# One Q projection per chunk for all four heads, spread to the heads' rows by way of DRAM

## The chip, the core and the metric

The kernel runs on one core of a Trainium2 chip. The metric is the device time of one execution in microseconds (us). Three runs of the kernel before took 6247.15, 6248.88 and 6250.07 us. A separate profiled execution gives the trace. The engines are called PE (TensorE), DVE (VectorE), ACT (ScalarE), POOL (GpSimd) and SP (SyncE, which issues nearly all DMAs).

## The reference

Two layers work on an image tensor of 4 images, 128 channels and 64 by 64 positions (4096 tokens an image).

```python
# layer 0: attention with 4 heads of 32 channels, residual, layer norm
Q, K, V = (split_heads(x_flat @ W + b) for W, b in ((Wq, bq), (Wk, bk), (Wv, bv)))
attn = softmax(einsum('bhnd,bhmd->bhnm', Q, K) * scale)
y = layernorm(einsum('bhnm,bhmd->bhnd', attn, V) @ Wo + bo + x_flat) * gamma + beta
# layer 1: the sum of three branches of y
spatial  = conv3x3(y) + bias
spectral = irfft2(channel_mix(rfft2(y)) + bias)
ym       = mamba(y)     # in_proj, causal conv of 4 taps, silu, a scan with 16 states, gate, out_proj
return spatial + spectral + ym
```

## The kernel before

**Tiling.** Tokens are handled in 32 chunks of 512 (8 an image). Attention goes by pairs of heads, so there are 64 halves H, each a chunk and a pair. A half takes 32 steps, one for each tile of 128 keys of the image, and a chunk 64 steps. The prediction calls these 64 steps a slot.

**One step of the hand-written loop.** For half H the kernel forms the scores of 128 keys against 512 queries (`scores_for_exp`, tile s, L478), subtracts the query's maximum by a matmul with `sel`, and takes the exponential on ACT (tile e, L486). The scores stand in one two-bank PSUM tile, so the matmuls of the next step wait until ACT has read it. In the same step PE forms scores of the next half for the running maximum (`scores_for_max`, L434, reduced by DVE into `part`, L441), seven steps ahead of their use, and multiplies the exponentials of the step before by V (`times_values`, L498).

**Precision.** Scores are single-pass matmuls of split numbers. Q is split into a high and a low part (tile Q, a [128, 2, 512] tile), K likewise. The rows of a pair are laid out as head, part, channel: two heads of 64 rows each, and within them 32 rows of K's high part and 32 of its low part. Q therefore has each head's 32 rows twice. The kernel before gets this layout from the weights: `wq_t` holds each head's columns twice, and one projection is made for each half.

**The Mamba scan** runs two chunks later, interleaved with attention. Every second step takes one vector of states: ACT makes the decay dA (L780), POOL the input term db (L785), DVE the scan hs (L793), and POOL copies the state, multiplies by C and accumulates (L796, L797, L812). The broadcast rows bc of B and C are loaded for each of the 16 states into three buffers (`scan_load`, L771).

**The planner.** All else (projections, convolution, gates, output) consists of generators, called jobs. A job is started by `plan.at(t, rank, job)` with the first step it may run. It asks for places by letters: P is a place for a matmul, D one on DVE, A one on ACT, B one of two spare PSUM banks; an empty string means only the next step. In the steady part an odd step has two places of P, D and A each, an even step a single place of A. Jobs are served by rank, then by their asked time. A job served earlier takes places from all behind it, so instructions of later jobs move to other steps.

**Jobs that the prediction names.** `project_q` makes Q (pq, L410; Q, L415 and L416). `project_kv` makes K and V of the next image (pk, L348; khi and klo; pv, L362; vst) and sends them by DRAM tiles kd and vd. `scan_dt` makes the step size: on ACT exponentials, logarithms and a bias (dt, spe, u, lnw), then on POOL three tensor operations (spe, dt, u, L738 to L740), and some steps later on ACT the scaling of xs by D (L747), which reads what the third POOL operation has read. `gate` makes the silu gate (pz, L756; zg). `scan_output` multiplies the accumulated scan by the gate on POOL (acc, L904) and, after two empty yields, projects it (py, L914). `flips` and `scan_output` add a mirrored image (L887).

[...]

Of the kernel before, what the change touches and what calls it, by code (L numbers as in the profile page):

```python
# [9 lines left out]
F32 = mybir.dt.float32  # L10
F32R = mybir.dt.float32r
AF = mybir.ActivationFunctionType
ALU = mybir.AluOpType
# [4 lines left out]
P = 128  # L18
W = 64
HEADS = 4  # L20
HD = P // HEADS
PAIRS = HEADS // 2
HS = P // 2
L = 512
# [131 lines left out]
def attention_then_conv_mamba(  # L156
# [38 lines left out]
    for h in range(HEADS):  # L195
        k, j = divmod(h, 2)
# [3 lines left out]
    for h in range(HEADS):  # L200
        k, j = divmod(h, 2)
        c = COL["bk"] + k
# [3 lines left out]
    Wk = wk_t.rearrange("c h d -> c (h d)")  # L206
    Wv = wat[:, 0, :]
    Wo = [wat[:, 1 + k, :] for k in range(PAIRS)]

    wq_t = const.tile([P, PAIRS, 2, 2, HD], F32, name="wq_t")  # L210
    bq = const.tile([P, PAIRS], F32, name="bq")
    for h in range(HEADS):
        k, j = divmod(h, 2)
        c = COL["bq"] + h
        for r in range(2):
            nc.scalar.dma_start(wq_t[:, k, j, r, :], wq[h, :, j * HS : j * HS + HD])
            nc.scalar.dma_start(
                bq[j * HS + r * HD : j * HS + (r + 1) * HD, k : k + 1],
                vecs[j * HS : j * HS + HD, c : c + 1],
            )  # L220
    Wq = [wq_t[:, k].rearrange("c j r d -> c (j r d)") for k in range(PAIRS)]
    nc.gpsimd.tensor_scalar(wq_t, wq_t, SCALE, None, ALU.mult)
    nc.gpsimd.tensor_scalar(bq, bq, SCALE, None, ALU.mult)
    cst = const.tile([P, K_SEL], F32, name="cst")
# [6 lines left out]
    for h in range(HEADS):  # L231
        row = h % 2 * HS
        hs = slice(h * HD, (h + 1) * HD)
# [19 lines left out]
    def col(name, k=0):  # L253
        return vec[:, COL[name] + k : COL[name] + k + 1]
# [5 lines left out]
    sel = const.tile([P, P], F32R, name="sel")  # L260
    ones = const.tile([P, 1], F32, name="ones")
    nc.vector.memset(ones, 1.0)
    minus_one = const.tile([P, 1], F32, name="minus_one")
    nc.vector.memset(minus_one, -1.0)
    g = const.tile([P, 3, P], F32, name="g")
# [53 lines left out]
    state = const.tile([P, NH * NS], F32, name="state")  # L319
# [5 lines left out]
    plan = Plan(2, {"x": 2, "f": 1})  # L325

    def bank_tile(bank, shape, name):
        return psum.tile(shape, F32, tag=f"m{bank}", name=name)


    def load_x(c, tag, bufs):
        t = att.tile([P, L], F32, tag=tag, name=f"{tag}_{c}", bufs=bufs)
        b, i = divmod(c, NCH)
        nc.sync.dma_start(t, x[b, :, i * L : (i + 1) * L])
        return t
# [61 lines left out]
    xqs = {}  # L397

    def load_q(c):
        yield ""  # L400
        xqs[c] = load_x(c, "xq", 2)

    def project_q(H):


        c, k = divmod(H, PAIRS)
        yield ""
        bank = yield "PB"
        pq = bank_tile(bank, [P, L], f"pq_{H}")
        nc.tensor.matmul(pq, Wq[k], xqs[c], start=True, stop=True)  # L410
        yield "DA"
        plan.release(bank, 2)
        q = att.tile([P, 2, L], F32R, tag="Q", name=f"Q_{H}", bufs=3)
        bias = bq[:, k : k + 1]
        nc.scalar.activation(q[:, 1, :], pq, AF.Identity, bias=bias)  # L415
        nc.vector.scalar_tensor_tensor(q[:, 0, :], pq, bias, q[:, 1, :], ALU.add, ALU.subtract)  # L416
        QT[H] = q


# [196 lines left out]
    def inner(c):  # L616
        return xps[c][:, 1 : RPC + 1, 1 : W + 1]

    def mamba_input(c):

        i = c % NCH
        while c not in XH:
            yield ""
        yield ""
        xp = loc.tile([P, RPC + 2, W + 2], F32, tag="xp", name=f"xp_{c}", bufs=2)
        xps[c] = xp
        nc.gpsimd.memset(xp[:, :, 0 : W + 2 : W + 1], 0.0)
        if i == 0:
            nc.gpsimd.memset(xp[:, 0, 1 : W + 1], 0.0)
            nc.gpsimd.memset(state, 0.0)  # L630
            nc.gpsimd.memset(carry, 0.0)
        if i == NCH - 1:
            nc.gpsimd.memset(xp[:, RPC + 1, 1 : W + 1], 0.0)
        bank = yield "PB"
        pt = bank_tile(bank, [P, TPC, P], f"pt_{c}")
        for t in range(TPC):
            nc.tensor.transpose(pt[:, t, :], XH[c][:, t, :], ident)
        yield "A"
        plan.release(bank)
# [127 lines left out]
    dA, db, bcs, scaled = {}, {}, {}, set()  # L767
# [19 lines left out]
    def scan_state(c, v):  # L787

        n, hf = divmod(v, NH)
        k = hf * NS + n  # L790
        assert (c, hf) in scaled
        hs = loc.tile([P, L], F32, tag="hs", name=f"hs_{c}_{k}")
        nc.vector.tensor_tensor_scan(  # L793
            hs, dA.pop((c, v)), db.pop((c, v)), state[:, k : k + 1], ALU.mult, ALU.add
        )
        nc.gpsimd.tensor_copy(state[:, k : k + 1], hs[:, L - 1 :])  # L796
        nc.gpsimd.tensor_tensor(hs, hs, bcs[c, n][:, 1, :], ALU.mult)  # L797
        if c >= CHUNKS - 2:

            if v == 0:  # L800
                late = psum.tile([P, NH, L], F32, tag=f"s{CHUNKS - c}", name=f"acc_{c}")
                for h in range(NH):
                    accs[c, h] = late[:, h, :]
            if n == 0:
                nc.tensor.matmul(accs[c, hf], ident, xss[c][hf], start=True, stop=False)
            nc.tensor.matmul(accs[c, hf], ident, hs, start=False, stop=n == NS - 1)  # L806
        elif n == 0:
            acc = loc.tile([P, L], F32, tag=f"acc{hf}", name=f"acc_{c}_{hf}")
            accs[c, hf] = acc
# [6 lines left out]
    def spectral(c):  # L816

        b, i = divmod(c, NCH)
        bank = yield "PB"
        p1 = bank_tile(bank, [P, TPC, P], f"p1_{c}")  # L820
        for t in range(TPC):
            nc.tensor.matmul(p1[:, t, :], XH[c][:, t, :], hilbert, start=True, stop=True)
        yield "A"
        plan.release(bank)
        hx = loc.tile([P, L], F32, tag="hx", name=f"hx_{c}", bufs=2)
        hxs[c] = hx
        nc.scalar.activation(
            hx, p1.rearrange("p t c -> p (t c)"), AF.Copy, scale=col("gamma")
        )
# [12 lines left out]
        if i == 0:  # L842
            wd[b] = dram.tile([P, N], F32, tag="wd", name=f"wd_{b}")
        nc.sync.dma_start(wd[b][:, i * L : (i + 1) * L], w)
# [106 lines left out]
    LEAD = 7  # L951
# [13 lines left out]
    plan.at(-4, 2, constants_of_the_rest())  # L965
    for H in range(HALVES):
        if H % PAIRS == 0:
            plan.at((H - 1) * NT - LEAD - 24, 0, load_q(H // PAIRS))
        plan.at((H - 1) * NT - LEAD - 14, 0, project_q(H))
        plan.at(H * NT - LEAD, 0, maxima(H))  # L970
        plan.at((H + 1) * NT + 1, 0, normalise(H, (H + 1) * NT + 9))
    for c in range(CHUNKS):
# [12 lines left out]
    while t < end or not plan.idle():  # L985
        H, m = divmod(t, NT)
# [5 lines left out]
        H, m = divmod(t - 1, NT)  # L992
# [3 lines left out]
        c, s = divmod(t - LAG, SLOT)  # L996
        odd = s % 2 == 1
        if -1 <= c < CHUNKS:
            v = c * STATES + s // 2
# [3 lines left out]
            else:  # L1003
# [8 lines left out]
                n = v // NH + 3  # L1012
# [87 lines left out]
```

## Time and profile before

| | |
|---|---|
| median of three runs | 6248.88 us |
| profiled execution, its own time | 6247.33 us |
| span of its trace | 6245.5 us |
| granted PE clock, mean | 0.978 |
| first exponential to last | 130.7 to 5967.6 us |
| instructions | 83489 |
| DMA bytes | 404.98 MB, 65 GB/s |

The first 130 us load weights, project K and V of the first image and find the first maxima. The main part has 2048 exponentials, so 2048 steps in 32 slots of 64. The last 280 us finish the scan and the output of the last chunks. The share of a busy engine is an average over these parts; what a change is worth is read from the step in which it lies. In the rows of groups, the numbers after the bar are the busy time, the mean of one instruction in ns, and the idle time of the engine just before them with what ended it. A two-pass f32 matmul shows as two records, so 64 projections are 128 records.

### The profile page before, as it was taken

The numbers are of one execution on the slowest core, as the hardware profiler recorded it, in microseconds if no ns is written. First come the engines' busy times: TensorE is split into PE (matmuls) and PEld (weight loads), VectorE is DVE, ScalarE is ACT, GpSimd is POOL, SyncE is SP. The second block draws the span as 40 slices with busy tenths as digits, with TensorE's granted clock in tenths as the row PEclk, the third lists the DMA queues.
The fourth block names the chain that finished last, engine by engine and source line by source line (L and its number), as shares of the span: only waits on it lengthen the run. The fifth ranks groups of instructions, "written<-read, shape, count | busy, mean of one in ns | idle before, by whom it ended". The sixth has DMA issues, their size and how long they took to land.

```text
span 6245.5 us, 83489 instructions
## 1 busy us (share of the span) xinstructions
PE 6001.6 (96%) x32076; PEld 2540.6 (41%) x32076; DVE 4284.2 (69%) x4405; ACT 3582.9 (57%) x4858; POOL 4605.3 (74%) x4951
## 2 busy tenths in 40 slices
PE   5999999999999999999999999999999999999956
PEld 2444444444444444444444444444444444444321
DVE  4556777777777677777767777767776766677556
ACT  1455666665666656566665556656565655665642
POOL 0006887777888777888887788877788877778866
PEclk7999999999999999999999999999999999999976
DMA  3002222223222222223232222222322222212223
GB/s 111 14 15 60 62 58 58 65 65 103 72 75 58 62 62 63 59 65 84 76 87 62 65 62 65 55 60 70 98 70 63 57 52 56 56 53 55 59 68 93
DMA packets 234225, 404.98 MB, mean 65 GB/s; under 512 B 38872, under 2 KB 40416, under 8 KB 233824
## 3 DMA queue, kind: packets, MB, share of 16 engines
q1 hardware_dynamic: 229440, 397.75, 23.3%
q8 instruction: 251, 4.11, 0.3%
q10 hardware_dynamic: 4384, 1.89, 0.1%
q14 instruction: 150, 1.23, 0.1%
HBM read 350.54 MB, written 49.02 MB: 64 GB/s over the span
## 4 chain that ended last, share of the span: by engine, by line
PE 80%; POOL 9%; DVE 5%; ACT 3%; issue 2%; DMA 1%; ACTq 0%; SPq 0%; POOLq 0%; DVEq 0%
PE po L498 27%; PE s L478 25%; PE s L434 13%; PE pf L857 4%; POOL hs L797 3%; DVE part L441 2%; ACT e L486 2%; DVE hs L793 2%; POOL db L785 1%; PE pi L663 1%; PE pdt L713 1%; POOL acc L812 1%; PE pq L410 1%; PE pd L699 1%; PE py L554 1%
## 5 line engine op out<-in xcount | busy, mean ns | idle before, releaser
L441 DVE TENSOR_REDUCE part<-s 128x2 f32<-128x1024 f32 x2048 | 2501.0, 1222 | 1613.6 <-PE s L434 1611.9
L486 ACT ACTIVATE e<-s 128x1024 f32<-128x1024 f32 x2048 | 2094.1, 1023 | 2257.5 <-PE s L478 2249.3
L498 PE MATMUL po<-e,V 128*33 128x512 f32 x8192 | 2160.1, 605 | 2.8 <-DVE oz L508 0.3
L478 PE MATMUL s<-Q,K 64*128 64x512 f32 x8192 | 1500.7, 444 | 25.3 <-ACT e L486 20.2
L793 DVE TENSOR_TENSOR_SCAN hs<-dA,state,db 128x512 f32<-128x512 f32 x1024 | 1305.7, 1275 | 158.9 <-ACT dA L780 69.2
L797 POOL TENSOR_TENSOR hs<-hs,bc 128x512 f32<-128x512 f32 x1024 | 1307.0, 1276 | 82.0
L434 PE MATMUL s<-K,Q 64*128 64x512 f32 x8192 | 1297.7, 395 | 44.4 <-DVE part L441 42.0
L478 PEld LDWEIGHTS s<-Q,K 64*128 64x128 f32 x8192 | 611.5, 185 | 1753.7 <-ACT e L486 1186.1
L785 POOL TENSOR_TENSOR db<-u,bc 128x512 f32<-128x512 f32 x954 | 1223.0, 1282 | 1.6 <-DMA bc<-bcd 1.6
L812 POOL TENSOR_TENSOR acc<-acc,hs 128x512 f32<-128x512 f32 x900 | 1151.7, 1280 | 70.6
L796 POOL COPY state<-hs 128x1 f32<-128x1 f32 x1024 | 212.6, 208 | 976.6 <-DVE hs L793 976.1
L434 PEld LDWEIGHTS s<-K,Q 64*128 64x128 f32 x8192 | 763.7, 186 | 280.5 <-DVE part L441 102.9
L478 PE MATMUL s<-MX,sel 64*128 64x512 f32 x4096 | 810.3, 392 | 0.0
L780 ACT ACTIVATE dA<-dt,negA 128x512 f32<-128x512 f32 x1024 | 702.5, 686 | 146.8 <-DVE hs L793 146.7
L498 PEld LDWEIGHTS po<-e,V 128*33 128x33 f32 x8192 | 299.2, 109 | 899.0 <-issue 865.0
L478 PEld LDWEIGHTS s<-MX,sel 64*128 64x128 f32 x4096 | 383.8, 184 | 90.0
L857 PE MATMUL pf<-xp,cw 128*128 128x512 f32 x576 | 288.2, 617 | 0.0
L450 POOL COPY wide<-mx 128x128 f32<-128x128 f32 x256 | 63.2, 292 | 196.9 <-DVE mx L447 196.9
L806 PE MATMUL acc<-hs,cst 128*128 128x512 f32 x128 | 110.8, 969 | 86.7 <-POOL hs L797 86.7
L531 POOL TENSOR_TENSOR oz<-oz,rz 128x512 f32<-128x512 f32 x64 | 81.9, 1279 | 106.7 <-DMA rz<-rd 106.7
L857 PEld LDWEIGHTS pf<-xp,cw 128*128 128x128 f32 x576 | 96.1, 188 | 131.9 <-issue 126.9
L554 PE MATMUL py<-wat_vo,oz 128*128 128x128 f32 x512 | 83.0, 285 | 22.6 <-POOL oz L531 18.6
(134 smaller groups left out, 3561.0 us busy)
## 6 DMA issues: line engine op xcount, KB each, us to landing
bc<-bcd SPq DMA_DIRECT2D x512, 512.0 KB
K<-kd SPq DMA_DIRECT2D x64, 256.0 KB
rz<-rd SPq DMA_DIRECT2D x128, 128.0 KB
vd<-vst SPq DMA_DIRECT2D x32, 264.0 KB
V<-vd SPq DMA_DIRECT2D x32, 264.0 KB
xq<-in_x SPq DMA_DIRECT2D x32, 256.0 KB
xk<-in_x SPq DMA_DIRECT2D x32, 256.0 KB
kd<-khi SPq DMA_DIRECT2D x32, 256.0 KB
```

Of the source, the lines that this page charges most:

```text
L434: nc.tensor.matmul(sc[:, j, :], QT[H][rows[j], n, t * P : (t + 1) * P], KK[k][m][rows[j], :], start=n == 0, stop=n == 1,)
L441: nc.vector.tensor_reduce(part[H][:, t, :, m], sc, AX.X, ALU.max)
L478: nc.tensor.matmul(s[:, j, :], sel[rows[j], :] if n == 2 else KK[k][i][rows[j], t * P : (t + 1) * P], mov[rows[j], :], start=n == 0, stop= ...
L486: nc.scalar.activation(e, s, AF.Exp)
L498: nc.tensor.matmul(po[H][used[j], :], VA[i][:, t, 2 * k + j, :], e[:, j, :], start=m == 0, stop=m == NT - 1,)
L780: nc.scalar.activation(dA[c, v], dts[c][hf], AF.Exp, scale=negA[:, k : k + 1])
L785: engine.tensor_tensor(db[c, v], us[c][hf], bcs[c, n][:, 0, :], ALU.mult)
L793: nc.vector.tensor_tensor_scan(hs, dA.pop((c, v)), db.pop((c, v)), state[:, k : k + 1], ALU.mult, ALU.add)
L796: nc.gpsimd.tensor_copy(state[:, k : k + 1], hs[:, L - 1 :])
L797: nc.gpsimd.tensor_tensor(hs, hs, bcs[c, n][:, 1, :], ALU.mult)
L812: nc.gpsimd.tensor_tensor(accs[c, hf], accs[c, hf], hs, ALU.add)
L857: nc.tensor.matmul(pf, cw[:, k, :], xps[c][:, dy : dy + RPC, dx : dx + W], start=k == 0, stop=False)
```

## The change

Q is projected once per chunk with the weights of all four heads side by side. The 128 rows of the result are the four heads. Its high part is taken on ACT and its low part on DVE, into the buffers that K's parts use (tags khi and klo). Both go to a DRAM tile `qd`. A second job, `place_q`, runs for each half and reads from `qd` into the tile Q: four DMAs of 32 partitions, each with both parts of a head. The projection is asked for at another step and once per chunk; the load of x moves with it. The weights and the bias are loaded once for each head instead of twice. Apart from this, the state of the scan isn't cleared on POOL any more; the first chunk of an image starts from a tile of zeros.

```diff
-    wq_t = const.tile([P, PAIRS, 2, 2, HD], F32, name="wq_t")
-    bq = const.tile([P, PAIRS], F32, name="bq")
+    wq_t = const.tile([P, HEADS, HD], F32, name="wq_t")
+    bq = const.tile([P, 1], F32, name="bq")
...
-        for r in range(2):
-            nc.scalar.dma_start(wq_t[:, k, j, r, :], wq[h, :, j * HS : j * HS + HD])
...
+        nc.scalar.dma_start(wq_t[:, h, :], wq[h, :, j * HS : j * HS + HD])
...
-    def project_q(H):
...
-        nc.tensor.matmul(pq, Wq[k], xqs[c], start=True, stop=True)
+    qd = {}
+    def project_q(c):
+        yield ""
+        bank = yield "PB"
+        pq = bank_tile(bank, [P, L], f"pq_{c}")
+        nc.tensor.matmul(pq, Wq, xqs[c], start=True, stop=True)
         yield "DA"
         plan.release(bank, 2)
+        hi = att.tile([P, L], F32R, tag="khi", name=f"qhi_{c}")
+        lo = att.tile([P, L], F32R, tag="klo", name=f"qlo_{c}")
+        nc.scalar.activation(hi, pq, AF.Identity, bias=bq)
+        nc.vector.scalar_tensor_tensor(lo, pq, bq, hi, ALU.add, ALU.subtract)
+        yield ""
+        qd[c] = dram.tile([2, HEADS, HD, L], F32, tag="qd", name=f"qd_{c}")
+        nc.sync.dma_start(qd[c][0].rearrange("h d l -> (h d) l"), lo.bitcast(F32))
+        nc.sync.dma_start(qd[c][1].rearrange("h d l -> (h d) l"), hi.bitcast(F32))
+
+    def place_q(H):
+        c, k = divmod(H, PAIRS)
+        while c not in qd:
+            yield ""
         q = att.tile([P, 2, L], F32R, tag="Q", name=f"Q_{H}", bufs=3)
-        bias = bq[:, k : k + 1]
-        nc.scalar.activation(q[:, 1, :], pq, AF.Identity, bias=bias)
-        nc.vector.scalar_tensor_tensor(q[:, 0, :], pq, bias, q[:, 1, :], ALU.add, ALU.subtract)
+        for j in range(2):
+            for r in range(2):
+                p0 = j * HS + r * HD
+                nc.sync.dma_start(
+                    q[p0 : p0 + HD].bitcast(F32), qd[c][:, 2 * k + j].rearrange("n d l -> d n l")
+                )
         QT[H] = q
...
-            nc.gpsimd.memset(state, 0.0)
...
-            hs, dA.pop((c, v)), db.pop((c, v)), state[:, k : k + 1], ALU.mult, ALU.add
+            hs,
+            dA.pop((c, v)),
+            db.pop((c, v)),
+            state[:, k : k + 1] if c % NCH else zero,
...
-            plan.at((H - 1) * NT - LEAD - 24, 0, load_q(H // PAIRS))
-        plan.at((H - 1) * NT - LEAD - 14, 0, project_q(H))
+            plan.at((H - 1) * NT - LEAD - 30, 0, load_q(H // PAIRS))
+            plan.at((H - 1) * NT - LEAD - 22, 0, project_q(H // PAIRS))
+        plan.at((H - 1) * NT - LEAD - 8, 0, place_q(H))
```

NT is 32 (steps of a half) and LEAD is 7.

More of the change, by code (lines that the diff above doesn't have):

```diff
@@ L214, in attention_then_conv_mamba @@
         c = COL["bq"] + h
-        for r in range(2):
-            nc.scalar.dma_start(wq_t[:, k, j, r, :], wq[h, :, j * HS : j * HS + HD])
[L217 to L221, printed above, removed]
+        nc.scalar.dma_start(wq_t[:, h, :], wq[h, :, j * HS : j * HS + HD])
+        nc.scalar.dma_start(
+            bq[h * HD : (h + 1) * HD, :], vecs[j * HS : j * HS + HD, c : c + 1]
+        )
+    Wq = wq_t.rearrange("c h d -> c (h d)")
     nc.gpsimd.tensor_scalar(wq_t, wq_t, SCALE, None, ALU.mult)
@@ L262, in attention_then_conv_mamba @@
     nc.vector.memset(ones, 1.0)
+    zero = const.tile([P, 1], F32, name="zero")
+    nc.vector.memset(zero, 0.0)
     minus_one = const.tile([P, 1], F32, name="minus_one")
@@ L401, in load_q @@
         xqs[c] = load_x(c, "xq", 2)
-    def project_q(H):
-        c, k = divmod(H, PAIRS)
+    qd = {}
+    def project_q(c):
         yield ""
         bank = yield "PB"
-        pq = bank_tile(bank, [P, L], f"pq_{H}")
-        nc.tensor.matmul(pq, Wq[k], xqs[c], start=True, stop=True)
+        pq = bank_tile(bank, [P, L], f"pq_{c}")
+        nc.tensor.matmul(pq, Wq, xqs[c], start=True, stop=True)
         yield "DA"
         plan.release(bank, 2)
-        q = att.tile([P, 2, L], F32R, tag="Q", name=f"Q_{H}", bufs=3)
-        bias = bq[:, k : k + 1]
-        nc.scalar.activation(q[:, 1, :], pq, AF.Identity, bias=bias)
-        nc.vector.scalar_tensor_tensor(q[:, 0, :], pq, bias, q[:, 1, :], ALU.add, ALU.subtract)
+        hi = att.tile([P, L], F32R, tag="khi", name=f"qhi_{c}")
[10 more added lines that the diff above has]
+            yield ""
+        q = att.tile([P, 2, L], F32R, tag="Q", name=f"Q_{H}", bufs=3)
+        for j in range(2):
[3 more added lines that the diff above has]
+                    q[p0 : p0 + HD].bitcast(F32), qd[c][:, 2 * k + j].rearrange("n d l -> d n l")
+                )
         QT[H] = q
@@ L793, in scan_state @@
         nc.vector.tensor_tensor_scan(
-            hs, dA.pop((c, v)), db.pop((c, v)), state[:, k : k + 1], ALU.mult, ALU.add
+            hs,
+            dA.pop((c, v)),
+            db.pop((c, v)),
+            state[:, k : k + 1] if c % NCH else zero,
+            ALU.mult,
+            ALU.add,
         )
```

## The prediction

> **What bounds the kernel now.** I read the page first: engine shares, then the chain of work that ended last.
>
> ```profile
> PE 6001.6 (96%) x32076; PEld 2540.6 (41%) x32076; DVE 4284.2 (69%) x4405; ACT 3582.9 (57%) x4858; POOL 4605.3 (74%) x4951
> PE 80%; POOL 9%; DVE 5%; ACT 3%; issue 2%; DMA 1%; ACTq 0%; SPq 0%; POOLq 0%; DVEq 0%
> ```
>
> TensorE is busy nearly always and 80% of the chain is its own. The groups, shapes kept apart, price what is removed.
>
> ```profile
> L410 PE MATMUL pq<-xq,wq_t 128*128 128x512 f32 x128 | 71.9, 644 | 0.0
> L416 DVE SCALAR_TENSOR_TENSOR Q<-pq,bq,Q 128x512 fp32r<-128x512 f32 x64 | 48.1, 751 | 51.1 <-ACT Q L415 51.0
> L415 ACT ACTIVATE Q<-pq,bq 128x512 fp32r<-128x512 f32 x64 | 43.5, 679 | 3.7 <-PE pq L410 3.7
> ```
>
> That alone would say "32 projections fewer, faster". Then I walked the timeline from one exponential (e, L486) to the next; each gap is one step of the hand-written loop, and 64 steps (one chunk of 512 tokens) I call a slot, numbered from 0. A step with no small matmul takes 2.34 us, with one 128x512 f32 projection 3.40 (so 1.06 us for one), with two 4.25. Slots repeat to 0.05 us, but there are two kinds. Here are a slot of the second image, one of the fourth, and the slot that starts at 565 us in the first (columns: stretch, length, busy time by engine, clock, DMA).
>
> ```profile
> 2290.28:2473.33 183.05, 182.27 (x1002) 78.07 (x998) 131.34 (x135) 111.37 (x152) 146.84 (x157) 1.00 0.24 62
> 4863.53:5050.11 186.58, 181.68 (x990) 76.20 (x988) 130.98 (x134) 111.32 (x151) 148.27 (x158) 1.00 0.21 56
> 565.35:753.25 187.90, 183.02 (x998) 77.38 (x994) 131.46 (x135) 110.46 (x150) 147.84 (x159) 1.00 0.23 60
> ```
>
> The fourth image's slot has less to do (no K, V projection for a next image: L348 1.06 and L362 1.08 us) and yet is 3.5 us longer. So about 5.6 us of it is stall. The first eleven steps show half of it: 26.97 against 30.87 us, of which one pz (L756) explains 1.06.
>
> ```profile
> 5060.79 1.28 POOL L740 TENSOR_TENSOR u<-dt,xs 128x512 f32<-128x512 f32 x1
> ...
> 5064.76 1.28 POOL L740 TENSOR_TENSOR u<-dt,xs 128x512 f32<-128x512 f32 x1
> ...
> 5064.11 0.71 ACT L747 ACTIVATE xs<-xs,vec 128x512 f32<-128x512 f32 x1
> 5066.06 0.72 ACT L747 ACTIVATE xs<-xs,vec 128x512 f32<-128x512 f32 x1 [1.24 <-POOL u L740]
> 5066.69 1.00 ACT L486 ACTIVATE e<-s 128x1024 f32<-128x1024 f32 x1
> ...
> 5067.75 0.74 PE L478 MATMUL s<-Q,K 64*128 64x512 f32 x4 [1.50 <-ACT e L486]
> ```
>
> In this kind of slot both halves of the step-size chain (spe, dt, u: L738 to L740, three POOL instructions of 1.28 us each) stand in step 0, six in a row, 7.7 us. Both xs scalings (L747) stand in ScalarE's queue in step 5, ahead of the exponential; the second waits for POOL's second u, the exponential behind it starts late, and TensorE idles 1.50 us for the bank that it frees. Step 5 takes 4.13 instead of 2.34 us. Behind the six, db and the scan are late too (steps 8 and 9: 3.09 and 3.53). The calm slot has the two halves in steps 4 and 10 and xs in steps 9 and 15: no such stall. I call the two kinds calm and bunched. The slot at 565 us is bunched too: 4.8 us longer than a calm one with the same matmuls.
>
> **What the Trainium skill says.** "Perfetto Trace Analysis", section Tensor Engine Instruction: ACT, DVE and GPSIMD queues are strict FIFO, and a matmul's end is modelled. The trace agrees on the first: the exponential, with its scores ready, starts only behind xs. So I take periods from ScalarE's starts, not TensorE's busy time. "DMA: Bandwidth & Descriptors", section Why a DMA increments its semaphore by 16 and not by 1: a transfer runs on the largest number of engines up to 16 that divides both outer sizes. So the new transfers (128 or 32 rows outermost) use 16. No view of this trace shows theirs; I use it only to split bytes evenly.
>
> **The change part by part.** The profiled execution took 6247.33 us, span 6245.5; the median of the runs is 1.55 us higher. I sum against the former and add 1.55.
>
> Removed: 32 projections (L410), 32 evictions on ScalarE (679 ns) and 32 on VectorE (751 ns). At 1.06 us a step the matmuls are worth 34 us where nothing else stalls. The evictions lie beside TensorE's work.
>
> Moved: the order of instructions by engine shows what the planner makes of it. The projection now asks at step 3 of a slot, earlier than any job around it, and takes matmul, vector and scalar places there; the second one (step 45) is gone. All jobs behind slide. In slots 4 to 23 the changed order is the bunched one: six POOL instructions in step 0, both xs in step 5. In slots 25 to 31 it is the spread one: halves in step 60 of the slot before and step 4, xs in steps 1 and 9. The kinds have changed places.
>
> (a) Slots 4 to 23, now bunched. From the fourth image's slot: 186.58, less two pq (2.12), plus K and V projection (2.14) is 186.6. From the slot at 565 us: 187.90 less two pq is 185.8. The new pq stands in step 5, inside the 1.50 us hole of TensorE, so I cost it at nothing; without that cover it costs 1.06. Its evictions stand in step 7, where ScalarE waits for a late scan anyway. I take 186.3 against 183.1: 3.2 more, 20 slots, **+64** (bounds 2.7 and 4.5: +54 to +90).
>
> (b) Slots 25 to 30, now calm: 183.1 less K, V and one pq (3.2), plus about 0.9 that the later steps keep (output projection waiting for POOL in step 21, convolution in 32 to 35) is 180.8, against 186.6: −5.8 each, −35. Slot 31 gives half, −3; slot 24 changes kind inside, +3. Sum **−35**. Slot 25, 189.2 before, may keep its extra.
>
> (c) Slots 9 and 17 add two rounds of flipped output (L887, 1.28 us each) to the bunch. In slot 25 before, that made py (L914) wait for POOL's gate product:
>
> ```profile
> 4733.87 3.78 PE L914 MATMUL py<-acc,outw 128*128 128x512 f32 x4 [2.75 <-POOL acc L904]
> ```
>
> That step took 10.0 us, against 4.7. py now stands at step 21 in every slot, three steps after the product, where it had five. So +5.3 each, **+10** (0 to 14).
>
> (d) Slots 0 to 3: one pq fewer each, **−4**.
>
> (e) Start. ScalarE's queue issues 8 DMAs fewer at 0.48 us (wq_t and bq, L216, L217), ahead of the first khi: −3.8. Against it, 1 MB of Q goes out and back ahead of kd and vd: 64 KB on each engine, 32 packets of 2 KB at 84 ns, 2.7 us for each direction, and the second khi waits for the buffer that the first Q write holds. One projection in the vector-bound stretch goes, about −1. I take **0** (−5 to +6).
>
> (f) Added DMAs: per chunk 2 writes and 8 reads, 320 issues on SP, 48 MB on 405. SP's own waits:
>
> ```profile
> SPq L771 <- POOL hs L797: 4183.6, 504, 31.3
> ```
>
> SP mostly stands at a bc load until POOL frees its buffer. An issue costs about 0.45 us there, and DMA engines are busy 24%: hidden by that wait. The new wait on SP is for qlo (step 7) and has bc loads behind it, which have two spare buffers (some 11 us). Reads stand 8 steps, some 23 us, ahead of the first score that needs them; SP runs at most 10 us behind in a bunched slot, and four issues and the landing need about 6. Cost 0; without the cover, what is missing is paid at each of 64 halves. The state memset goes (4 times 0.13 us on POOL): 0.
>
> Sum: 64 − 35 + 10 − 4 + 0 = +35, 6282 on the profiled execution, **6284** on the median.
>
> **The rivals.** First, faster: the bunch does not stall, because ScalarE and POOL have slack elsewhere and TensorE catches up; then only matmuls count, 6248.9 − 34 = 6215. For it: TensorE's 96%. Against it: all seven bunched slots of this trace (3 and 26 to 31) stall in step 5. It decides where POOL's six instructions end before ScalarE reaches the second xs, 1.24 us sooner than now: below that the stall is gone in the 20 slots. Second, partial: the bunch stalls about half as long (the smaller eviction load in steps 15 to 17 helps), 1.5 a slot instead of 3.2, 34 less: 6250, no change that a measurement of this kernel can tell, which is about 0.2% or 12.5 us. Third, slower still: Q's reads land late. With SP 10 us behind, the margin is 23 − 10 − 6 = 7 us; once used up, each further microsecond costs 64 over the kernel, 5 late would give 6600. SP's lag speaks against it. That the change does nothing is excluded: the order has 32 pq and 256 reads of Q.
>
> **How the numbers follow.** Forecast 0.78, first rival 0.08, second 0.10, third 0.04. Faster by over 0.2% is the first, 0.08; within 0.2% the second, 0.10; slower the rest, 0.82. Range: the bounds of (a), (c), (e) together give 6265 to 6318; I go down to the second rival's edge, 6254, and up to 6314.
>
> **What would show it.** Slots 4 to 23 at about 186.3 us and slots 26 to 30 at about 180.8; a longer total of ACT xs waiting for POOL u (23.8 us in 11 waits before, to some 40 in over 25); TensorE busy down about 34 us with a longer span; DMA share up by two or three points; scores never waiting for a Q read. Wrong would be: slots of 182 us in the first three images (the bunch is harmless), or scores (L434 before) waiting for DMA.

## The result, and the profile after

The kernel after takes 6310.97 us (median of five runs, 6310.32 to 6314.88), the kernel before 6249.77 us beside it: ratio 1.0098, 95% interval 1.0086 to 1.0111. It is slower by 61 us; 35 us were predicted. The profiled execution took 6310.95 us, its span 6309.2.

The page of the kernel after: engine shares, then the chain of waits by engine.

```profile
PE 6010.5 (95%) x32012; PEld 2515.4 (40%) x32012; DVE 4269.0 (68%) x4374; ACT 3588.4 (57%) x4826; POOL 4606.5 (73%) x4947
PE 70%; POOL 14%; DVE 8%; issue 4%; ACT 3%; DMA 1%; ACTq 0%; SPq 0%; POOLq 0%; DVEq 0%
```

There are 64 matmul records fewer (32 projections), and yet TensorE is busy for 9 us longer. Its share of the chain fell from 80% to 70%, POOL's rose from 9% to 14% and DVE's from 5% to 8%: more of the work now waits for these two. What was to be saved was saved, as the groups of pq and its two evictions show (busy time, mean ns, idle before with its releaser):

```profile
L409 PE MATMUL pq<-xq,wq_t 128*128 128x512 f32 x64 | 37.0, 660 | 12.0 <-POOL wq_t L219 12.0
L415 DVE SCALAR_TENSOR_TENSOR qlo<-pq,bq,qhi 128x512 fp32r<-128x512 f32 x32 | 24.0, 751 | 27.2 <-ACT qhi L414 27.2
L414 ACT ACTIVATE qhi<-pq,bq 128x512 fp32r<-128x512 f32 x32 | 21.5, 672 | 16.9 <-DMA cw<-in_conv_w 16.9
```

The slots, from one exponential's start to the one 64 steps later, show where the time went. Slots 12 and 27 of the kernel after, to be held against the calm slot of before at 2290.28 us and the bunched one at 4863.53 us (stretch, length, busy time by engine, clock, DMA share, GB/s):

```profile
2325.49:2513.53 188.04, 183.38 (x998) 77.13 (x996) 131.08 (x134) 112.14 (x153) 146.90 (x157) 1.00 0.24 68
5135.95:5318.32 182.37, 181.11 (x990) 75.90 (x986) 130.36 (x133) 110.24 (x150) 147.02 (x156) 1.00 0.26 65
```

The two kinds did change places: the slot of the second image is now the long one, 5.0 us longer than before, and the slot of the fourth image is 4.2 us shorter. Summed from the exponentials' starts, and set against the steps of the prediction:

| part | before | after | predicted | measured |
|---|---|---|---|---|
| slots 4 to 23, (a) and (c) | 3669.2 | 3763.9 | +74 | +94.7 |
| slots 24 to 31, (b) | 1475.7 | 1446.9 | −35 | −28.8 |
| slots 0 to 3, (d) | 692.1 | 689.8 | −4 | −2.3 |
| to the first exponential, (e) | 130.7 | 129.9 | 0 | −0.9 |
| after the last exponential's start | 277.9 | 278.7 | 0 | +0.8 |

The stall in step 5 is there as foretold. A part of the timeline of slot 12, whose step 5 starts at 2338.03 us (start, length, engine, line, tiles, idle before it):

```profile
2336.21 1.27 POOL L756 TENSOR_TENSOR u<-dt,xs 128x512 f32<-128x512 f32 x1
...
2338.34 1.13 PE L409 MATMUL pq<-xq,wq_t 128*128 128x512 f32 x2
...
2340.16 1.29 POOL L756 TENSOR_TENSOR u<-dt,xs 128x512 f32<-128x512 f32 x1
...
2341.48 0.72 ACT L763 ACTIVATE xs<-xs,vec 128x512 f32<-128x512 f32 x1 [1.21 <-POOL u L756]
...
2342.11 1.01 ACT L503 ACTIVATE e<-s 128x1024 f32<-128x1024 f32 x1
...
2343.17 0.73 PE L495 MATMUL s<-Q,K 64*128 64x512 f32 x4 [0.37 <-ACT e L503]
```

The second xs waits 1.21 us for the second u. The exponential is behind it, and the step takes 4.08 us although it has a projection: pq lies in TensorE's hole, of which 0.37 us are left, and costs nothing there. But a later step had not been expected to grow. Step 21 of the same slot, on POOL and on TensorE:

```profile
2382.41 1.29 POOL L831 TENSOR_TENSOR acc<-xs,hs 128x512 f32<-128x512 f32 x1
2383.65 2.50 POOL L925 TENSOR_TENSOR acc<-acc,zg 128x512 f32<-128x512 f32 x2
```

```profile
2384.98 2.35 PE L935 MATMUL py<-acc,outw 128*128 128x512 f32 x4 [0.97 <-POOL acc L925]
```

POOL goes from one operation to the next without a pause; TensorE idles 0.97 us before py and, for a moment, between its two halves. The step takes 5.68 us, against 4.73 in the bunched slots of the kernel before. The waits say the same in sum (total us, times, longest):

```profile
PEld py L935 <- POOL acc L925: 57.6, 58, 1.4
ACT xs L763 <- POOL u L756: 37.2, 24, 9.0
```

```profile
SPq L787 <- POOL hs L818: 4157.6, 505, 23.7
```

The wait of py was 14.6 us in 16 times before, that of xs 23.8 in 11. SP's wait at the bc load is as long as before (4183.6).

The 5.0 us of slot 10, in three parts with equal jobs but for one pq less in the last: steps 0 to 20 took 55.36 us and take 58.23 (+2.9); steps 21 to 39, 51.49 and 53.62 (+2.1); steps 40 to 63, 76.20 and 76.17, so that nothing is left of the 1.06 us of the pq removed there. Besides, a step with no small matmul (a plain step) takes 2.360 us where it took 2.340, by the medians of slots 4 to 23.

### The profile page after: what moved, and what is told of

The parts are those of the page before. It is cut to its first block, busy times and chain, and to the rows that moved or that the text cites. A ratio compares the mean times of both kernels' runs of the same rounds, so it can differ in the third digit from the quotient of the medians.

```text
span 6309.2 us, 83680 instructions
## 1 busy us (share of the span) xinstructions
PE 6010.5 (95%) x32012; PEld 2515.4 (40%) x32012; DVE 4269.0 (68%) x4374; ACT 3588.4 (57%) x4826; POOL 4606.5 (73%) x4947
## 4 chain that ended last, share of the span: by engine, by line
PE 70%; POOL 14%; DVE 8%; issue 4%; ACT 3%; DMA 1%; ACTq 0%; SPq 0%; POOLq 0%; DVEq 0%
PE po L515 23%; PE s L495 21%; PE s L451 12%; PE pf L878 4%; POOL hs L818 4%; DVE part L458 3%; DVE hs L809 3%; POOL db L801 2%; ACT e L503 1%; POOL acc L833 1%; PE pdt L729 1%; PE pi L679 1%; POOL u L756 1%; POOL dt L755 1%; PE py L571 1%
## 5 line engine op out<-in xcount | busy, mean ns | idle before, releaser
L451 PE MATMUL s<-K,Q 64*128 64x512 f32 x8192 | 1328.9, 402 | 74.9 <-DVE part L458 70.5
L809 DVE TENSOR_TENSOR_SCAN hs<-dA,state,db 128x512 f32<-128x512 f32 x896 | 1142.9, 1276 | 175.5 <-ACT dA L796 74.0
L451 PEld LDWEIGHTS s<-K,Q 64*128 64x128 f32 x8192 | 752.8, 185 | 343.5 <-DVE part L458 174.2
L809 DVE TENSOR_TENSOR_SCAN hs<-dA,zero,db 128x512 f32<-128x512 f32 x128 | 163.2, 1275 | 6.1 <-POOL db L801 5.9
```

Of the source, the lines that this page charges most:

```text
L451: nc.tensor.matmul(sc[:, j, :], QT[H][rows[j], n, t * P : (t + 1) * P], KK[k][m][rows[j], :], start=n == 0, stop=n == 1,)
L809: nc.vector.tensor_tensor_scan(hs, dA.pop((c, v)), db.pop((c, v)), state[:, k : k + 1] if c % NCH else zero, ALU.mult, ALU.add,)
```

## The experiments

Four theories were to be told apart. B: six POOL operations in a bunch hold xs, and with it the exponential. G: py stands too close behind POOL's gate product. A: the tiles moved in memory (the smaller wq_t and the new zero tile shift all that lies behind them), which lengthens the plain steps. D: the transfers to Q cost what A is blamed for. Late a fifth was added, P: POOL's queue as a whole sets the pace of steps 0 to 21. Times are medians; the ratio is to the kernel before on the same chip.

| kernel | us | ratio, 95% interval | slots 4 to 23, median | slots 26 to 30, mean |
|---|---|---|---|---|
| before | 6249.77 | 1 | 183.1 | 186.6 |
| after | 6310.97 | 1.0098 (1.0086 to 1.0111) | 188.1 | 182.4 |
| 1 after, halves spread | 6254.33 | 1.0007 (0.9999 to 1.0016) | 185.7 | 182.4 |
| 2 after, no DRAM trip | 6296.21 | 1.0076 (1.0061 to 1.0091) | 187.7 | 182.0 |
| 3 after, 32 bytes of padding | 6295.79 | 1.0075 (1.0060 to 1.0090) | 187.5 | 181.8 |
| 4 before, Q asked for earlier | 6290.54 | 1.0067 (1.0051 to 1.0084) | 186.2 | 183.6 |
| 5 after, py two steps later | 6303.77 | 1.0083 (1.0066 to 1.0100) | 186.9 | 182.6 |
| 6 after, edits 1, 3 and 5 | 6213.91 | 0.9939 (0.9924 to 0.9953) | 182.8 | 182.1 |
| 7 before, 32 bytes of padding | 6268.18 | 1.0027 (1.0017 to 1.0036) | 183.7 | 187.1 |
| 8 after, padding behind K and V | 6298.20 | 1.0073 (1.0058 to 1.0088) | 187.7 | 182.0 |
| 9 as 2, trip as a dead load | 6298.13 | 1.0075 (1.0058 to 1.0092) | 187.7 | 182.0 |
| 10 before, edits 1 and 5 | 6218.63 | 0.9948 (0.9933 to 0.9963) | 183.1 | 181.9 |
| 11 as 6, py two more steps later | 6221.63 | 0.9955 (0.9940 to 0.9970) | 183.8 | 183.0 |
| 12 after, zg on DVE | 6296.61 | 1.0075 (1.0059 to 1.0092) | 187.2 | 182.4 |

The intervals of neighbouring kernels overlap in places. The smaller differences rest on the slots, which repeat to about 0.05 us within an execution; between executions, run 10, which leaves the order of the calm slots as it was, has the same median of 183.09 us as the kernel before.

**1. The halves spread.**

```diff
         for hf in range(NH):
-            plan.now(1, scan_dt(c, hf, xd))
+            plan.at(plan.t + 6 * hf, 1, scan_dt(c, hf, xd))
```

> The kernel after, with one line changed: the second half of the POOL work that makes dt and u is asked for six steps later than the first, so that slots 4 to 23 run calm (POOL halves in steps 0 and 8, xs in steps 5 and 13) and everything else stands as in the kernel after. Theory B (the bunch): six POOL operations in step 0 hold both xs and all that is behind them on ACT; without the bunch slots 4 to 23 fall from 188.0 us to 183.5 to 185 us, and the time to 6225 to 6255 us; the step in which py follows the gate product (step 21, 5.65 us) stays above 4.5 us only if its wait is not a sequel of the bunch. Rival G (the gate): the loss is in py standing three steps after POOL's gate product and in the longer plain steps; then slots 4 to 23 stay above 187 us and the time above 6290 us.

6254.33 us: 57 us are gone with this one line. That isn't the whole loss of the slots: of the 94.7 us by which slots 4 to 23 had grown, 53.7 are gone and 41 stay, and the shorter slots 24 to 31 make up for most of these in the total. Slots 6 and 12 of this kernel:

```profile
1188.63:1247.32 58.69, 57.55 (x330) 25.25 (x330) 44.77 (x52) 39.03 (x52) 53.87 (x56) 1.00 0.32 80
2299.28:2484.95 185.67, 182.77 (x997) 77.25 (x997) 131.43 (x134) 111.97 (x151) 146.84 (x157) 1.00 0.28 69
```

Slot 12 is 2.4 us shorter than in the kernel after, others 3.4. The median of 185.7 us is just above theory B's 183.5 to 185, the time just within its range; rival G's ranges are far off. The first line is the stretch of slot 6 up to the end of its gate product; what it shows is taken up under run 12. The step with py is still at 5.66 us in slot 12, so its wait is no mere sequel of the stall in step 5.

**2 and 9. The DRAM trip.** In run 2 ACT and DVE write Q directly, and the rows of the heads aren't rearranged; in run 9 the trip is put back beside it, into a tile that nothing reads.

```diff
-        hi = att.tile([P, L], F32R, tag="khi", name=f"qhi_{c}")
-        lo = att.tile([P, L], F32R, tag="klo", name=f"qlo_{c}")
+        q = att.tile([P, 2, L], F32R, tag="Q", name=f"Q_{c}", bufs=3)
+        hi, lo = q[:, 1, :], q[:, 0, :]
...
-        qd[c] = dram.tile([2, HEADS, HD, L], F32, tag="qd", name=f"qd_{c}")
-        nc.sync.dma_start(qd[c][0].rearrange("h d l -> (h d) l"), lo.bitcast(F32))
-        nc.sync.dma_start(qd[c][1].rearrange("h d l -> (h d) l"), hi.bitcast(F32))
+        qd[c] = q
...
-        q = att.tile([P, 2, L], F32R, tag="Q", name=f"Q_{H}", bufs=3)
...
-        QT[H] = q
+        QT[H] = qd[c]
```

> The kernel after, with the way by DRAM taken out: ACT and DVE write the two parts of the projected Q straight into a Q tile that both head pairs of the chunk then use, so the rows of the heads are not rearranged (that part of the computation is changed: the head order in Q is not that of the reference) and 6 DMAs and 1.5 MB per chunk are gone, while TensorE, ACT, DVE and POOL have the same instructions in the same order. Theory B with A (bunch and addresses): no change, 6305 to 6317 us, plain steps 2.355 us. Rival D (the transfers): writes to Q by DMA or the busier queue lengthen every step; then plain steps fall back to 2.335 us and the time to 6270 to 6285 us, or lower if the transfers also cause part of the stall.

> The run without the DRAM trip, with the trip put back as a dead load: the two parts of Q go to DRAM and are read back by the same DMAs on the same queue, into a tile that nothing reads; Q itself is still taken as ACT and DVE wrote it (the rows of the heads are not rearranged, as there), and the buffers behind Q lie where they lay. Theory D (the transfers cost the 15 us): back to 6305 to 6317 us, plain steps 2.355 us. Theory A (the place of Q in memory, which differs from the kernel after, gave the 15 us): 6291 to 6300 us, plain steps 2.341 us.

Run 2 gave 15 us, with plain steps of 2.347 us: between the two forecasts, so that it decides nothing alone. Run 9, with the transfers back, kept the whole gain. Slot 12 of run 2, then of run 9:

```profile
2317.13:2504.80 187.67, 182.86 (x998) 77.40 (x996) 130.89 (x134) 112.03 (x153) 146.84 (x157) 1.00 0.21 60
2319.01:2506.63 187.62, 182.80 (x998) 77.38 (x996) 130.85 (x134) 112.02 (x153) 146.85 (x157) 1.00 0.28 69
```

The DMA share goes from 0.21 to 0.28 and the length doesn't move. The transfers cost nothing in the slots, and D falls. What is left to explain the gain of run 2 is where the tiles lie (by the order in which tiles are asked for, Q comes ahead of khi, klo and vst and not behind them, and so 10304 bytes lower), or that engines and not DMAs write Q. The Trainium skill says in "SBUF — State Buffer", section Who interferes with whom, that a DMA doesn't contend with a compute engine; these two lines, 187.67 and 187.62 us, agree.

**3, 7 and 8. Where the tiles lie.**

```diff
# run 3
-    zero = const.tile([P, 1], F32, name="zero")
+    zero = const.tile([P, 9], F32, name="zero")[:, :1]
# run 7, in the kernel before
-    ones = const.tile([P, 1], F32, name="ones")
+    ones = const.tile([P, 9], F32, name="ones")[:, :1]
# run 8: behind K and V
-    carry = const.tile([P, NH, TAPS - 1], F32, name="carry")
+    carry = const.tile([P, NH, TAPS + 3], F32, name="carry")[:, :, : TAPS - 1]
```

> The kernel after, with 32 bytes of padding in the small constant pool: every tile behind it moves up by 32 bytes, so that the K tiles start at a multiple of 64 bytes again as in the kernel before, and the e and Q tiles at 32 more than one, as before. Nothing else differs. Theory A (addresses): the 16 to 20 ns by which every plain step is longer than before comes from where the tiles lie; plain steps fall from 2.355 to 2.335 us, every slot by about 1.1 us, the time to 6272 to 6284 us. Rival D (the transfers, or something else that came with the change): no change, 6305 to 6317 us.

> The kernel before, with 32 bytes of padding in the small constant pool and nothing else: K moves from a multiple of 64 bytes to 32 more, Q and e the other way, as in the kernel after. Theory A (placement alone lengthens the steps): plain steps from 2.335 to about 2.355 us, slots 0.5 to 1.1 us longer, 6262 to 6285 us. Rival: placement costs only together with the transfers to Q that the kernel after has; then 6246 to 6254 us.

> The kernel after, with 32 bytes of padding behind the K and V tiles: K and V stay where the kernel after has them, all buffers of attention and of the scan (Q, part, e, dt, bc and so on) move up by 32 bytes, to where the run with 32 bytes in the constant pool had them. If the place of K or V is what matters: no change, 6305 to 6317 us, plain steps 2.355 us. If the place of the buffers that are written all the time (e, Q, part, the scan) matters: 6291 to 6299 us, plain steps 2.336 us.

Padding alone took 15 us off the kernel after, and put 16.5 us on the kernel before, whose instructions and their order it leaves as they are. The plain step went to 2.335 us in run 3 and to 2.354 in run 7, as theory A said. In run 7 the slots (+0.65 us) and the time lie in its ranges; in run 3 the slots moved by half of what it said (−0.55 us) and the time lies between its range and its rival's. The group of the scores for the maximum (busy time, mean ns) in before, after, run 3 and run 7:

```profile
L434 PE MATMUL s<-K,Q 64*128 64x512 f32 x8192 | 1297.7, 395 | 44.4 <-DVE part L441 42.0
```

```profile
L451 PE MATMUL s<-K,Q 64*128 64x512 f32 x8192 | 1328.9, 402 | 74.9 <-DVE part L458 70.5
```

```profile
L451 PE MATMUL s<-K,Q 64*128 64x512 f32 x8192 | 1311.1, 398 | 76.5 <-DVE part L458 71.4
```

```profile
L434 PE MATMUL s<-K,Q 64*128 64x512 f32 x8192 | 1323.0, 400 | 41.8 <-DVE part L441 39.8
```

The same 8192 matmuls are busy 18 us less with the padding in the kernel after, and 25 us more in the kernel before. Run 8 leaves K and V where the kernel after has them and moves only the buffers behind; it is still 13 us faster than that kernel. So K and V needn't move for the gain. Which of the buffers matters, and by what mechanism, stays open.

**4. The order without the rest.** The kernel before, its own two projections a slot, asked for earlier.

```diff
-            plan.at((H - 1) * NT - LEAD - 24, 0, load_q(H // PAIRS))
-        plan.at((H - 1) * NT - LEAD - 14, 0, project_q(H))
+            plan.at((H - 1) * NT - LEAD - 30, 0, load_q(H // PAIRS))
+        plan.at((H - 1) * NT - LEAD - 22, 0, project_q(H))
```

> The kernel before, with only the moment changed at which Q is asked for: each pair still has its own projection, one step earlier in the queue of each pair than the change needs (22 steps ahead instead of where it was), no DRAM, the same tiles at the same addresses. The slots keep POOL's halves eight steps apart, in steps -2 and 6, and py comes three steps after the gate product as in the kernel after. Theory B: no bunch, so slots 4 to 23 stay within 182 to 185 us, slots 26 to 30 come down from 186.6 to about 181 to 183 us, time 6225 to 6265 us; plain steps 2.335 us. Rival M (moving the projection away from step 15 is in itself what costs, since something else fills or empties that place): slots 4 to 23 at 187 us or more, time above 6300 us.

6290.54 us, between the two forecasts: theory B alone is wrong here. There is no bunch, and yet slots 4 to 23 take 186.2 us, 3.1 more than before. With 1.06 us for each projection that moved from one part to another, of slot 10's +3.2 some 2.2 lie in steps 21 to 39 (the step with py, 21, takes 5.74 us) and 1.5 in steps 40 to 63; steps 0 to 20 are half a microsecond shorter. So an early projection costs without any bunch. A part of it is that scan_output comes in steps 18 to 21 and no longer in 26 to 31, and py waits there for POOL; the 1.5 us weren't taken apart. (7.6 us of this run's time are lost before the first exponential, which starts at 138.4 us.)

**5. py two steps later.**

```diff
-        yield ""
-        yield ""
+        for _ in range(4):
+            yield ""
         bank = yield "PB"
         pf = bank_tile(bank, [P, L], f"py1_{c}")
```

> The kernel after, with two more empty steps in the output job between POOL's gate product and py: py moves from step 21 to step 23, pt from 23 to 21; the bunch stays. Theory G (the gate is the second term: py stands three steps behind the product in slots 4 to 30, and waits for it): the step with py falls from 5.60 to 4.3 to 4.7 us, every slot by 0.9 to 1.3 us, the time from 6311 to 6275 to 6288 us. Rival S (the wait has slack behind it, or POOL is so late that two steps don't help): slots within 0.3 us of the kernel after, time above 6303 us.

7 us, a miss. The step with py did fall to 4.27 us, what two projections cost without a wait; but the slots fell by only 1.1 us in 4 to 6, 11 to 14 and 19 to 22, and not at all in 7, 8, 10, 15, 16, 18 and 23. These are slots with flipped output. And slots 24 to 31 grew by 6.5 us together. Step 27 of slot 10 (it starts at 2019.70 us), on POOL and TensorE:

```profile
2019.63 1.25 POOL L908 TENSOR_TENSOR ob<-ob,wr 128x504 f32<-128x504 f32 x1
...
2021.00 0.98 POOL L467 COPY wide<-mx 128x128 f32<-128x128 f32 x4
```

```profile
2021.34 1.02 PE L474 MATMUL pm<-cst,wide 128*128 128x128 f32 x4 [1.26 <-POOL wide L467]
```

The additions of the flipped output follow py, so they came later too and now stand just ahead of `wide`, for which pm waits: in these slots one wait took the place of another.

**6, 10 and 11. The edits together, and the same for the kernel before.** Run 6 is the kernel after with edits 1, 3 and 5. Run 10 is the kernel before with edits 1 and 5. Run 11 is run 6 with six empty yields instead of four.

> The kernel after, with three edits at once: the second half of the step-size work six steps later (no bunch), py two steps later, and 32 bytes of padding in the constant pool. If the three terms are separate losses they add: 6311 - 57 (bunch) - 15 (placement) - 25 to -35 (gate) = 6204 to 6214 us, below the kernel before; slots 4 to 23 at about 182.8 us, slots 26 to 30 at about 180.7. If they share one slack (one wait takes the place of another), the time stays above 6230 us.

> The kernel before, with the second half of the step-size work six steps later and py two steps later: its own bunched slots 3 and 26 to 30 are spread, the calm ones keep their order. If the bunch and the gate cost there what they cost in the kernel after: slots 3 and 26 to 30 fall by 3 to 4.5 us each, time 6222 to 6236 us; then of the 38 us by which the kernel with three edits beats the kernel before some 10 to 22 are the change's own, the projections saved. If the kernel before gains nothing from it, above 6244 us.

> The kernel with three edits, with py a further two steps later (step 25). In slots 7 to 10, 15 to 18 and 23 of the kernel with three edits the flipped output's POOL additions stand ahead of wide, and pm waits in step 27: 184.1 instead of 182.7 us. If that is the cause, they fall to 182.7 to 183.2 and the time to 6196 to 6206 us; if POOL's backlog only moves on, they stay at 184 and the time at 6210 us or more.

Run 6 took 6213.91 us, 0.6% below the kernel before; slots 4 to 23 took 182.8 us as expected, slots 26 to 30 182.1 where 180.7 had been expected. The three terms more than add: 57, 15 and 7 alone are 79, together they are 97. Of the 94.7 us by which slots 4 to 23 had grown they take 89.2. If the first two keep their worth, py's place is worth some 25 once the bunch is gone, as had been expected. But run 10 gets nearly all of it without the change: 6218.63 us, just below the range that was expected. That is 4.7 us more than run 6, where 10 to 22 had been expected for the change itself, and the intervals of the two ratios overlap. In slots 4 to 23 run 10 is even the shorter one, 3667.5 us against 3674.7. So the version with Q projected once isn't shown to be better than the one with two projections when both have a good order. Slot 12 of run 6, then slots 12 and 27 of run 10:

```profile
2286.07:2468.83 182.76, 181.71 (x996) 77.30 (x996) 130.01 (x134) 111.69 (x152) 146.81 (x157) 1.00 0.27 70
```

```profile
2286.31:2469.39 183.08, 182.31 (x1002) 78.07 (x998) 131.32 (x135) 111.38 (x153) 146.85 (x157) 1.00 0.22 61
5038.76:5220.37 181.61, 180.79 (x988) 76.44 (x988) 131.37 (x135) 110.56 (x150) 146.94 (x156) 1.00 0.21 56
```

With a projection fewer, slot 12 is 0.3 us shorter and not 1.06. In slot 11, steps 21 to 39 are 0.8 us longer in run 6 than in the kernel before with the same matmuls. py isn't the cause, its step takes 4.26 us; steps 32 to 35 take 10.43 us with no small matmul in them, where they took 10.34 with one, and in step 34 TensorE waits 0.47 us for DVE. And its slots with flipped output stay 1.3 us above the others. Slot 9 stays 5.5 above: pm waits 3.1 us for POOL there, and the granted clock in the 6 us after that wait was 0.53. Run 11 was to mend that, and the time rose: pm moved to step 28, an even step, by itself, and still waits for POOL there (the step takes 4.47 us). Of slots 4 to 23 the flipped ones fell from 184.1 to 183.8, slot 9 too, and all others rose to 183.8. The expectation that the flipped ones would reach 182.7 was wrong; the other branch, that POOL's backlog only moves on, is what came.

**12. A POOL operation to DVE.** The gate product ends 60.66 us after the start of slot 12 in the kernel after, and 60.65 us after that of slot 27 in the kernel before; both slots are bunched. The stretches up to it, of after and of before:

```profile
2325.49:2386.15 60.66, 56.73 (x326) 24.51 (x324) 45.98 (x53) 37.64 (x50) 54.81 (x57) 1.00 0.27 78
```

```profile
5050.11:5110.76 60.65, 56.43 (x326) 24.57 (x324) 45.74 (x53) 37.62 (x50) 55.09 (x58) 1.00 0.25 65
```

In runs 2 and 3, with shorter plain steps, it ends at 60.60 and 60.61. In all of these POOL pauses only twice for longer than 0.3 us, near 2 and 43 us. Where the halves are spread it ends at 58.7 us in slot 6 (the line shown with run 1) and 59.8 in slot 12. That suggests a limit by POOL, which run 12 tries.

```diff
-            nc.gpsimd.tensor_tensor(z, z, a, ALU.mult)
+            nc.vector.tensor_tensor(z, z, a, ALU.mult)
             gates[c][hf] = z
```

> The kernel after, with one POOL operation of each gate half moved to DVE: zg times its sigmoid (1.3 us on POOL, once in steps 0 to 21 and once later), the order otherwise the same, the bunch kept. Theory P (in slots 4 to 23 POOL's unbroken queue sets when py in step 21 can run: the gate product ends 60.6 to 60.7 us after the start of the slot in the bunched slots of both kernels): with one operation less it ends at 59.3 to 59.5, these slots fall by 0.9 to 1.3 us to 186.8 to 187.1, the time to 6283 to 6294 us. Rival X (the stall of ACT at xs and TensorE set the length of that stretch, and POOL has slack in it): slots within 0.3 us of 188.05, time 6303 to 6317 us.

The gate product ends at 59.80 us, 0.86 sooner, and slots 4 to 24 (but for 9) fall by just that, to 187.2. py runs without a wait, and step 21 takes 4.32 us instead of 5.68:

```profile
2380.34 2.04 PE L935 MATMUL py<-acc,outw 128*128 128x512 f32 x4
```

The gate product had been expected at 59.3 to 59.5 us. The run's 6296.61 us lies 2.6 above the range of theory P and well below that of its rival; the gain is 14 us and not 17 to 28, because 0.5 us came back in steps 8 to 20. One place of it is seen on POOL, 39 us into the slot, where it waits for the scan on DVE (0.17 us in the kernel after):

```profile
2360.26 0.18 POOL L817 COPY state<-hs 128x1 f32<-128x1 f32 x1 [0.96 <-DVE hs L809]
```

So POOL's queue does set the length of steps 0 to 21 in a bunched slot, up to a point: once it is 0.9 us shorter, the other engines are the limit. "Perfetto Trace Analysis", section Optimizing Scalar/DVE Operations, says that moving work between GPSIMD and DVE might not help because they share an SBUF read port; here one operation of 1.3 us moved so brought 0.9 a slot.

## Why the prediction was right, point by point

The direction and the exchange of the two kinds of slot held, and (a), (b) and (d) have the sign that was forecast. The sum came out 28 us too small (35 against 63.5 in the table). That the time still lies in the range, 3 us below its edge, is in part luck: (a) went beyond its own bound of +90, and (c), which was to add 10, didn't come.

- **(a), mis-sized.** The term "186.58, less two pq (2.12), plus K and V projection (2.14) is 186.6", with 185.8 from the other slot, was too low: the slots took 188.05, and the 4.9 us more than before lie beyond the bound of 4.5. Only one pq, that of step 45, could be taken off. The one of step 15 stood in the stretch that POOL sets: the first 22 steps took 63.81 us in the bunched slot of before and 63.82 in slot 12 of after, with the same number of matmuls. The new pq lay in the hole as was said, but the removed one had been in a hole of the same queue, and its time turned into the longer wait of py (5.68 for 4.73 us). 186.58 − 1.06 + 2.14 is 187.7; run 3, with 32 bytes of padding, has 187.5. The other 0.55 us is the place of the tiles, for which the prediction had no term. That the bunch is a part of why these slots are long is shown by run 1. It isn't all of it: runs 4 and 12 show POOL's queue ahead of py as a second part, and no run takes the whole apart.
- **(b), mis-sized.** −28.8 instead of −35. Slots 26 to 30 took 182.4 instead of 180.8; 0.6 of that is the place of the tiles (run 3: 181.8). The 0.9 kept in steps 21 to 39 is what came; the remaining 1.0 lies for the most part in steps 40 to 63 (step 43 takes 2.62 us with no job in it), and no run took it apart. Slot 25 is 0.7 us longer than its neighbours, for the most part in step 15 (3.20 us for 2.63); its extra of 2.6 before was something else, see (c).
- **(c), failed.** Slots 9 and 17 are 1.4 us longer than their neighbours, as they were before, so the 10 us didn't come. The step that failed is the price: the 5.3 us by which step 21 of slot 25 of before was longer than its like were put on a bunched slot as a longer wait for POOL. But the gate product of slot 25 ended 60.66 us after the start of the slot, as in the bunched slots behind it (60.65 in slot 27). Step 21 was longer for two other reasons. Slot 25 isn't bunched, so TensorE came to that step at 56.4 us and not at 59.1, and had 2.7 us longer to wait. And from 4733.8 to 4740.5 us, after that wait, the granted clock was 0.53. Run 7, which has the same order, shows the step at full clock:

```profile
4749.87 2.35 PE L914 MATMUL py<-acc,outw 128*128 128x512 f32 x4 [2.70 <-POOL acc L904]
```

Its py takes 2.35 us and not 3.78, its step 21 takes 7.41 us and not 10.01, and its slot 25 is as long as slots 26 to 30 (187.1 us). In the kernel after, the extra of slot 9 lies in step 7 (5.23 us for 3.85), where the first flipped addition stands; the gate product then ends 1.4 us later than in slot 10, step 21 begins as much later, and py's step is as long (5.60 us in both).
- **(d), right by luck.** −2.3 for −4. Slots 0 to 2 didn't get shorter by a pq each but longer by 1.4 us together, and slot 3 is 3.8 us shorter: it was bunched before and isn't now, which (d) left out.
- **(e), right in the sum alone.** −0.9 for 0. The wait of khi for the buffer that the first Q write holds is there, 3.2 us. But the first exponential starts at 129.9 us in the kernel after and at 133.5 in run 3, which differs by padding alone, so the parts aren't confirmed.
- **(f), right.** The transfers cost nothing in the slots; run 9 shows it. The share of DMA queue 1 rose from 23.3 to 26.0%, no score waited for a Q read, and SP's total at the bc loads stayed. The DMAs moved 50.3 MB more; 48 were counted.
- **The rivals.** The first needed the bunch not to stall; it does. What it promised, 34 us for 32 projections, doesn't come with a good order either: run 6 lies 4.7 us below run 10. The second, half a stall, is excluded by the slots of 188 us, and the third, late reads of Q, by (f).
- **The signs to look for.** The wait of xs rose as foretold (37.2 us in 24). TensorE's busy time went up by 9 us, where 34 less was expected: its busy time holds the longer modelled matmuls of the shifted tiles (31 us more in L451 alone), so it isn't a measure of removed work.
- **Slips in the working.** The stretch from 565.35 to 753.25 us isn't a slot. The bunched slot of the first image is slot 3, which starts at 634.95 us; its length of 187.90 us is right, the busy times shown beside it are those of another stretch. The first eleven steps took 26.94 and 30.80 us, not 26.97 and 30.87. And the bounds of (a), (c) and (e) add up to 6257 to 6318, not 6265 to 6318. The estimate and the range stay as they are with these.

## What to carry to other kernels

In a kernel with a hand-written order, moving one job moves all that are served after it: price a change by the order that it leaves, slot by slot, and not by the operations that it saves. Before taking a removed instruction off a slot, ask which queue sets the end of the stretch in which it stood; where that is another engine's unbroken queue, the removal only lengthens a wait. A step taken as a price should be held against a second run of the same order: the 10.0 us behind (c) held a slow clock of that one execution. And when two kernels differ in a tile's size, try each with a few bytes of padding too: here that alone was a quarter of the difference.

## What the runs showed of the hardware that was not expected

Thirty-two bytes of padding changed the time of this kernel by 15 us one way and 16.5 us the other (runs 3 and 7), at equal instructions: 14 to 25 ns in a plain step, seen in the fp32r score matmuls (395 to 402 ns in the mean). It isn't the place of K and V alone (run 8), and the transfers play no part in it (run 9). The Trainium skill's "SBUF — State Buffer", section Operand start alignment, states from which addresses an operand may start, not that the place changes the pace; no run here shows the mechanism.

TensorE's granted clock often fell after a long wait. In the fourteen traces TensorE idled for over 2 us inside the slots eleven times. In the 6 us after eight of these waits (2.2 to 3.1 us) the mean granted clock was 0.50 to 0.72, after the other three (2.2 to 2.7 us) it was 1.00. After the 18 of 1.5 to 2 us it fell four times, after the 577 of 0.6 to 1.5 us never; nine further falls stand where TensorE didn't wait. So the length of the wait alone doesn't decide it, and no run here shows what does.
